# A graph layer's source rows: one tile in 64 fetched row by row by SyncE instead of by an indirect DMA of GpSimd

## The chip, the cores and the metric

One core of a Trainium2 chip. The metric is the device time of one execution in microseconds, the median of several; beside it stands one profiled execution with its trace.

## What is computed

One message-passing layer over a graph of 12,500 nodes (64 features) and 212,500 edges (32 features), sorted by destination, with a residual and a layer norm. All is float32:

```python
msg_in = concatenate([nodes[row], nodes[col], edge_features], axis=-1)
messages = relu(msg_in @ mW1 + mb1) @ mW2 + mb2
aggregated = segment_sum(messages, col, num_segments=12500)
upd = relu(concatenate([nodes, aggregated]) @ uW1 + ub1) @ uW2 + ub2
out = layernorm(nodes + upd)
```

`row` (the kernel's `src`) is in no order; `col` (`dst`) rises along the edges. So what belongs to the destinations lies in a narrow window of nodes for a stretch of edges, and what belongs to the sources has to be gathered.

## The kernel before

The edges are cut into 554 groups (G) of 384 edges, three tiles of 128 each (TG = 3). Of each group the kernel needs the source rows x[src], one edge to a partition, in `own_s`, a ring of RING = 20 groups in SBUF; the edge features in `own_st`, transposed, one block to four groups (SB = 4); and a window of 32 rows of a table of destinations (`by_dst`, made on the chip in the first steps) in `own_wm`, a ring of eight.

The loop over k (lines 617 to 662) is one step of a software pipeline. TensorE does three things in step k as one block of matmuls, with one wait ahead of it (`step`, line 586):
- `turn(k)` (372): it transposes the three tiles of group k from `own_s` into PSUM (L378). It waits for the group's gathers and for the one-hot columns. ScalarE then copies the result into `own_st` (L389).
- `hidden(k-2)` (399): the first layer of the messages (L404), from `own_st` and `own_wm`; VectorE takes the relu into `own_h` (L415).
- `sums(k-4)` (425): the segment sums by one-hot matmuls (L431), and counts (L442); VectorE adds them into `agg` (L458) and `xc` (L463).

The order on each engine is the order in which the code calls for it; nothing is rescheduled. The engines meet through semaphores alone.

The source rows come in two ways. **GpSimd** issues one indirect DMA per tile (`gather`, line 164, L167), 16 groups ahead in the order of the code. Before it overwrites a slot of the ring it waits for the transpose of the group that had the slot (`turn_by[g - RING]`). It has no other work in the loop. **VectorE and ScalarE** spare it the first tile of 180 groups (COPIED): they copy single columns of 64 features from x^T, which lies whole in SBUF, into `own_st`, 20 columns a step on VectorE (L565) and 24 on ScalarE (L567), at addresses loaded into registers (L546) from a list of indices (L525). So a group has three gathers or, one time in three, two: 1481 in all.

**SyncE** issues the other DMAs from one queue, in order, and an instruction that waits holds up all behind it. In step k these are, in this order: every fourth step the edge features of a later block (`inputs`, 312, L316), which wait for the step k-1 of TensorE; the output of a finished block of nodes, one step in 21 or so (L516), which waits for VectorE; `window(k + 4)` (347), the rows of `by_dst` for group k+4 at an address from a register (L358; every fourth step it loads four registers first, L353), which waits for TensorE's step k-2; every eighth step a list of column indices (L525). Until step 24 it also writes `by_dst`, block by block (L344).

Of the kernel before, what the change touches and what calls it, by code (L numbers as in the profile page):

```python
# [12 lines left out]
I32 = mybir.dt.int32  # L13
# [3 lines left out]
ET = mybir.EngineType  # L17
# [3 lines left out]
P = 128  # L21
N = 12500
E = 212500
D = 64
# [6 lines left out]
TG = 3  # L31
GE = TG * P
G = (E + GE - 1) // GE
SB = 4
AHEAD = 16
RING = AHEAD + 4
BLOCKS = 3
NW = 2 * SB
COUNT = 96
# [7 lines left out]
SHORT = 10  # L47
LEAD = 6
TIMES = 4
BEGIN = 18  # L50
# [2 lines left out]
ACOLS = (12, 12)  # L53
COLS = sum(VCOLS + ACOLS)
SPAN = 8


def tiles_of(g):

    n = min(GE, E - g * GE)  # L60
    return [min(P, n - j * P) for j in range((n + P - 1) // P)]
# [23 lines left out]
COPIED = []  # L85
while BEGIN - (-P * (len(COPIED) + 1) // COLS) < G - SHORT:
    COPIED.append(BEGIN - (-P * (len(COPIED) + 1) // COLS))


class Own:  # L90
# [24 lines left out]
def ordered(ctx: ExitStack, tc: tile.TileContext, a, own, ok):  # L115
# [3 lines left out]
    nc = tc.nc  # L119
    x, out = a["x"], a["out"]  # L120
# [5 lines left out]
    ixp = ctx.enter_context(tc.tile_pool(name="index", bufs=2))  # L126
# [10 lines left out]

    loads, places_by, copy_by, relu_by, sums_by, wm_by, turn_by = ({} for _ in range(7))
    efs_by, hidden_by, counted_by = {}, {}, {}
    columned = set(COPIED)  # L140

    def after(first, *others):

# [20 lines left out]
    def gather(g):  # L164
        s = own.s[g % RING]
        loads[g] = [
            nc.gpsimd.indirect_dma_start(  # L167
                out=s[:p, j, :D], out_offset=None, in_=x[:, :],
                in_offset=bass.IndirectOffsetOnAxis(
                    ap=src_sb[:p, g * TG + j : g * TG + j + 1], axis=0),  # L170
            )
            for j, p in enumerate(tiles_of(g)) if j or g not in columned
        ]
        for i in loads[g]:
            after(i, *([turn_by[g - RING]] if g >= RING else []))

# [93 lines left out]
    wc = const.tile([H, H], F32, name="wc")  # L270

    starts, rows_at, indices, columns_by = {}, {}, {}, {}
    by_dst = dram.tile([NP, H], F32, name="by_dst")
    written = []

# [71 lines left out]
    def window(g):  # L347

        if g >= G:
            return  # L350
        if g % SB == 0:
            n = min(SB, G - g)
            _, v = nc.values_load_multi_w_load_instructions(  # L353
                start_i[0:1, g : g + n], engines=[ET.SP], min_val=0, max_val=N - 1,
                skip_runtime_bounds_check_because="they were clamped to the nodes on the chip",
            )
            rows_at.update(zip(range(g, g + n), v))
        wm_by[g] = nc.sync.dma_start(wm[g % NW][D : D + W, :],  # L358
                                     by_dst[bass.ds(rows_at.pop(g), W), :])
        after(wm_by[g], *written, *([hidden_by[g - NW]] if g >= NW else []))  # L360
        written.clear()
# [10 lines left out]
    def turn(g, ps):  # L372


        s = own.s[g % RING]
        xt = ps[0][: D + W, :GE]
        did = [
            nc.tensor.transpose(xt[:, j * P : j * P + p], s[:p, j, :], ident[:p, :p])  # L378
            for j, p in enumerate(tiles_of(g))
        ]  # L380

        def copy(step):
            t, c, n = columns(g)
            turn_by[g] = step
            whole = [(slice(D + W), slice(n))]
            apart = [(slice(D, D + W), slice(P)), (slice(D + W), slice(P, n))]
            copies = [
                ordered_by_steps(
                    after(nc.scalar.activation(t[r, c : c + n][:, m], xt[r, m], AF.Copy), step))  # L389
                for r, m in (apart if g in columned else whole)  # L390
            ]
            if g >= BLOCKS * SB:
                after(copies[0], hidden_by[g - BLOCKS * SB])
            copy_by[g] = copies
            return copies

        return did, [*loads.pop(g), places_by[g]], copy

    def hidden(g, ps):
        t, c, n = columns(g)  # L400
# [67 lines left out]
    def update(base, p, n):  # L468

        rows, q = slice(base, base + p * n), p * n  # L470

        def inner():
            u_ps = ups.tile([H, CH], F32, name="u_ps")
            nc.tensor.matmul(u_ps[:, :q], wc, agg[:, rows], start=True, stop=False)
            nc.tensor.matmul(u_ps[:, :q], ux, xc[: COUNT + 1, rows], start=False, stop=True)
            return u_ps

        def relu(u_ps):
            u = up.tile([H, CH], F32, name="u")
            nc.scalar.activation(u[:, :q], u_ps[:, :q], AF.Relu)  # L480
            return u

        def outer(u):
            y = ups.tile([H, CH], F32, name="u_ps")[:, : 4 * D].rearrange("p (n d) -> p n d", n=4)
            for k in range(n):
                at = k * p
                nc.tensor.matmul(y[:p, k], xc[: D + 1, base + at : base + at + p], same,  # L487
                                 start=True, stop=False)
                nc.tensor.matmul(y[:p, k], u[:, at : at + p], u2, start=False, stop=True)  # L489
            return y  # L490

        def stats(y):
            parts = up.tile([P, 4, nc.vector.BN_STATS_DIM], F32, name="stats")
            mv = up.tile([P, 4, nc.vector.BN_AGGR_DIM], F32, name="mv")
            for k in range(n):
                nc.vector.bn_stats(parts[:p, k], y[:p, k])
                nc.vector.bn_aggr(mv[:p, k], parts[:p, k])
            return y, mv

        def root(ym):  # L500
            y, mv = ym
            rstd = up.tile([P, 4], F32, name="rstd")
            nc.scalar.activation(rstd[:p, :n], mv[:p, :n, 1], AF.Sqrt, bias=eps[:p])
            return y, mv, rstd

        def scaled(ymr):
            y, mv, rstd = ymr
            nc.vector.reciprocal(rstd[:p, :n], rstd[:p, :n])
            o = up.tile([P, 4, D], F32, name="o")
            for k in range(n):  # L510
                nc.vector.tensor_scalar(
                    o[:p, k], y[:p, k], mv[:p, k, 0:1], rstd[:p, k : k + 1],
                    ALU.subtract, ALU.mult,
                )
            queue = nc.scalar if base + q == N else nc.sync
            queue.dma_start(out[rows, :].rearrange("(n p) d -> p n d", p=p), o[:p, :n])  # L516

        return [inner, relu, outer, stats, root, scaled]

    def indexes(i):  # L520

        n = min(SPAN * COLS, P * len(COPIED) - i * SPAN * COLS)
        if n > 0:
            indices[i] = ixp.tile([1, SPAN * COLS], I32, name="index")
            nc.sync.dma_start(indices[i][:, :n], a["src_copied"][:, i * SPAN * COLS :][:, :n])  # L525

# [26 lines left out]
    def fetch(*parts):  # L553

        for part in parts:
            engine, c0, v = held.pop(part, (None, 0, ()))
            for q, at in enumerate(v, c0):
# [8 lines left out]
                else:  # L566
                    by[engine] = nc.scalar.activation(o, x_at, AF.Copy)  # L567
                ordered_by_steps(after(by[engine],
                                       *([hidden_by[g - BLOCKS * SB]] if new else [])))

    waiting = [(closes, update(base, p, n)) for base, p, n, closes in PLAN]
    now = []

# [37 lines left out]
    for g in range(SB):  # L611
        window(g)
    indexes(0)
    made = summed = 0
    between, held = [], {}

    for k in range(G):
        if k < BITS:
            bit(k)
        if 1 < k < len(TABLE):  # L620
            projected(k)
        if k == CHECKED:
            addresses(0)
            combined()
            ordered_edges()
            early.close()
            up = ctx.enter_context(tc.tile_pool(name="upd", bufs=2))
        if k % SB == 2:
            inputs(k // SB + 2)
        if k % SB == 1:  # L630
            places(k // SB + 1)
        if k < G - SHORT:
            between.append(lambda: registers(k, 0))
            step((turn, k), *([(hidden, k - 2)] if k > 1 else []),
                 *([(sums, k - 4)] if k > 3 else []))
            made, summed = max(0, k - 1), max(0, k - 3)
            if between:
                between.pop()()
            fetch(0)
        else:  # L640

            step((turn, k))
            for _ in range(2):
                if summed < made:
                    step((sums, summed))
                    summed += 1
            for _ in range(2):
                if made <= k:
                    step((hidden, made))
                    made += 1  # L650
        window(k + SB)
        onehot(k + LEAD)
        if k < G - SHORT:
            for part in range(1, len(VCOLS + ACOLS)):
                registers(k, part)
                fetch(part)
            if k >= BEGIN and (k - BEGIN) % SPAN == 0:
                indexes((k - BEGIN) // SPAN + 1)
            if k >= BEGIN and (k - BEGIN) % SPAN == SPAN - 2:
                addresses((k - BEGIN) // SPAN + 1)  # L660
        if k + AHEAD < G:
            gather(k + AHEAD)
# [330 lines left out]
```

## Time and profile before

| | us |
|---|---|
| median of 3 runs | 1879.1 (1875.58 to 1879.48) |
| the profiled execution | 1872.44 |
| its span, first to last instruction | 1870.6 |

Busy shares of that span: TensorE's matmuls 70%, its weight loads 61%, VectorE 78%, ScalarE 83%, GpSimd 75%; mean granted TensorE clock 0.952. The 16 DMA engines were busy for a quarter of the time through most of the span. How to read it: no engine is near 100%, since each has gaps that the page lists as idle time with what ended them; issuing a DMA, loading registers and waiting on SyncE count as no busy time at all, so SyncE has no row among the engines and must be looked up in the waits, by source line and in the timeline.

### The profile page before, as it was taken

To read this page: it belongs to the slowest core of one execution; us is meant where nothing else is said; L and a number is where in the kernel's file an instruction comes from. 1 tells how busy PE (TensorE), PEld (TensorE's weight loads), DVE (VectorE), ACT (ScalarE), POOL (GpSimd) and SP (SyncE) were. 2 spreads that over 40 slices of the span, in tenths; PEclk is the share of its full clock that TensorE was granted. 3 is DMA by queue.
4 is the path that set the end of the run, shared out by engine and by line. 5 is a ranking of instruction groups with operands and counts; after the bars stand their busy time and mean duration, and the time that the engine had idled before them with its cause. 6 is when DMAs were issued, how large, how long until landed. Compare 5 with 4: busy or idle time off the path is not lost. (4 is left out here: it accounts for less than half of the span.)

```text
span 1870.6 us, 55967 instructions
## 1 busy us (share of the span) xinstructions
PE 1302.0 (70%) x9839; PEld 1139.3 (61%) x9839; DVE 1452.9 (78%) x13141; ACT 1558.7 (83%) x13374; POOL 1400.1 (75%) x1488
## 2 busy tenths in 40 slices
PE   1777777677767667677676776776767767667676
PEld 0676666666666556566665666665656656556665
DVE  1338888899897888877887878888878888888773
ACT  5249999999998888888888888888888888888871
POOL 7777777777777777777777777777777777777774
PEclk9889999999999998998999998999998999999999
DMA  4543222222222222222222222222222222222221
GB/s 93 138 123 75 54 54 54 51 54 53 52 54 48 50 52 49 50 49 45 54 52 47 52 46 54 48 51 48 53 46 53 45 54 51 48 53 48 50 49 26
DMA packets 112796, 104.10 MB, mean 56 GB/s; under 512 B 51586, under 2 KB 82960, under 8 KB 112432
## 3 DMA queue, kind: packets, MB, share of 16 engines
q0 software_dynamic: 47392, 48.60, 14.8%
q1 hardware_dynamic: 64196, 51.35, 10.0%
q14 instruction: 280, 2.29, 0.4%
q8 instruction: 84, 1.38, 0.3%
q10 hardware_dynamic: 844, 0.48, 0.1%
HBM read 90.61 MB, written 9.62 MB: 54 GB/s over the span
## 5 line engine op out<-in xcount | busy, mean ns | idle before, releaser
L167 POOL DMA_INDIRECT own_s<-in_x,src_sb x1481 | 1399.4, 945 | 452.5 <-issue 342.9
L567 ACT ACTIVATE own_st<-own_xc 64x4 uint8 x12560 | 1265.6, 192 | 60.2 <-issue 52.2
L565 DVE COPY own_st<-own_xc 64x4 uint8 x10480 | 884.5, 190 | 17.3 <-issue 9.2
L378 PE MATMUL own_ps<-own_ident,own_s 128*96 128x128 f32 x1661 | 294.1, 288 | 488.7 <-DMA own_s<-in_x,src_sb 164.0
L378 PEld LDWEIGHTS own_ps<-own_ident,own_s 128*96 128x96 f32 x1661 | 169.1, 131 | 593.5 <-issue 291.0
L431 PE MATMUL own_ps<-own_s,own_h 128*128 128x128 f32 x3322 | 490.3, 287 | 1.2 <-DVE own_h L415 0.6
L404 PE MATMUL own_ps<-own_wm,own_st 128*128 128x128 f32 x3322 | 485.5, 285 | 0.0
L415 DVE TENSOR_SCALAR own_h<-own_ps 128x384 f32<-128x384 f32 x553 | 302.1, 547 | 185.5 <-PE own_ps L442 84.7
L431 PEld LDWEIGHTS own_ps<-own_s,own_h 128*128 128x128 f32 x3322 | 443.3, 203 | 2.3 <-DVE own_h L415 1.2
L404 PEld LDWEIGHTS own_ps<-own_wm,own_st 128*128 128x128 f32 x3322 | 437.8, 201 | 1.8 <-issue 1.2
L389 ACT ACTIVATE own_st<-own_ps 96x384 f32<-96x384 f32 (+2 forms) x734 | 294.2, 401 | 167.5 <-PE own_ps L442 81.6
L458 DVE TENSOR_TENSOR own_agg<-own_ps,own_agg 128x32 f32 x554 | 105.8, 191 | 170.6 <-DVE own_h L415 90.4
L366 DVE TENSOR_TENSOR own_s<-iota,dlc 128x96 f32<-128x96 f32 x554 | 136.2, 247 | 0.3 <-issue 0.2
L442 PE MATMUL own_ps<-own_s,own_one 128*1 128x128 f32 x834 | 120.6, 283 | 0.0
L463 DVE TENSOR_TENSOR own_xc<-own_ps,own_xc 1x32 f32 x554 | 101.9, 184 | 18.5 <-DVE own_xc L463 1.8
L442 PEld LDWEIGHTS own_ps<-own_s,own_one 128*1 128x1 f32 x834 | 60.2, 85 | 35.7 <-issue 3.6
L340 PE MATMUL u_ps<-w1b,own_xc 65*128 65x128 f32 x196 | 33.4, 323 | 58.1 <-ACT t L343 38.8
L340 PEld LDWEIGHTS u_ps<-w1b,own_xc 65*128 65x128 f32 x196 | 29.1, 227 | 62.3 <-ACT t L343 42.1
L343 ACT ACTIVATE t<-u_ps 128x512 f32<-128x512 f32 (+1 forms) x25 | 14.7, 588 | 58.2 <-DMA by_dst<-t 37.9
L487 PE MATMUL u_ps<-same,own_xc 65*128 65x64 f32 (+1 forms) x196 | 37.0, 271 | 1.5 <-ACT u L480 1.4
L489 PE MATMUL u_ps<-u,u 128*128 128x64 f32 (+1 forms) x196 | 38.0, 276 | 0.0
L487 PEld LDWEIGHTS u_ps<-same,own_xc 65*128 65x128 f32 (+1 forms) x196 | 29.7, 191 | 2.3 <-ACT u L480 2.2
(62 smaller groups left out, 257.1 us busy)
## 6 DMA issues: line engine op xcount, KB each, us to landing
own_st<-in_efT SPq DMA_DIRECT2D x138, 192.0 KB
own_s<-in_x,src_sb POOLq DMA_INDIRECT x1481
own_wm<-by_dst SPq DMA_DIRECT2D x554, 16.0 KB
by_dst<-t SPq DMA_DIRECT2D x24, 256.0 KB
out<-o SPq DMA_DIRECT2D x24, 128.0 KB
own_xc<-in_xT SPq DMA_DIRECT2D x12, 179.2 KB
index<-in_src_copied SPq DMA_DIRECT2D x65, 1.4 KB
dlc_i<-in_dst_cols SPq DMA_DIRECT2D x1, 831.0 KB
```

Of the source, the lines that this page charges most:

```text
L167: nc.gpsimd.indirect_dma_start(out=s[:p, j, :D], out_offset=None, in_=x[:, :], in_offset=bass.IndirectOffsetOnAxis(ap=src_sb[:p, g * TG + ...
L366: places_by[g] = nc.vector.tensor_tensor(own.s[g % RING][:, :, D:], iota.unsqueeze(1).to_broadcast([P, TG, W]), dlc[:, g * TG : (g + 1) * ...
L378: nc.tensor.transpose(xt[:, j * P : j * P + p], s[:p, j, :], ident[:p, :p])
L389: after(nc.scalar.activation(t[r, c : c + n][:, m], xt[r, m], AF.Copy), step))
L404: nc.tensor.matmul(pre[:p, j, :], t[:, c + j * P : c + j * P + p], wm[g % NW], start=True, stop=True)
L415: relu_by[g] = [nc.vector.tensor_scalar(h, pre, 0.0, None, ALU.max)]
L431: did.append(nc.tensor.matmul(sg, h[:p, j, :], s[:p, j, D:].unsqueeze(1).to_broadcast([p, TIMES, W]), start=j == 0, stop=j == len(sizes) - 1))
L442: did.append(nc.tensor.matmul(at_ps[:, : len(whole)], own.one, own.ring[:, first_s : first_s + len(whole), j, D:], start=j == 0, stop=j == ...
L458: did = [after(nc.vector.tensor_tensor(agg[:, at], sg[:, 0, :], agg[:, at], ALU.add), step)]
L463: did.append(after(nc.vector.tensor_tensor(count, counted, count, ALU.add), step))
L565: by[engine] = nc.vector.tensor_copy(o, x_at)
L567: by[engine] = nc.scalar.activation(o, x_at, AF.Copy)
```

## The change

Of 24 groups (41, 62, 83, 105, ..., 531: BY_ROWS) the last tile is no longer gathered by GpSimd. SyncE fetches its 128 rows, 256 bytes each, one DMA to a row, six in a step (ROWS_A_STEP), from step 18 on. The group whose rows were issued last in some step is used two steps later (ROW_LEAD). The address of each row comes from a register; every second step SyncE loads twelve registers (PAIR) from a list of indices, which is fetched anew every 16 steps. In step k all of this comes behind `window(k + 4)`. The first row of a group waits for the transpose of the group that had the slot; as rows of one group are fetched over 21 to 22 steps ahead, the ring goes from 20 to 24 groups. The transposes of such a group wait for its rows too. In the built program each row is a pair of an address calculation and a DMA, as each fetch of `window` is, and the order of the other instructions on SyncE stays.

```diff
-RING = AHEAD + 4
+RING = 24
...
+ROWS_A_STEP = 6
+PAIR = 2 * ROWS_A_STEP
+ROW_SPAN = 8 * PAIR
+ROW_LEAD = 2
...
+BY_ROWS = []
+while True:
+    last = BEGIN + (P * (len(BY_ROWS) + 1) - 1) // ROWS_A_STEP
+    if last + ROW_LEAD >= G - SHORT:
+        break
+    BY_ROWS.append(last + ROW_LEAD)
...
-            for j, p in enumerate(tiles_of(g)) if j or g not in columned
+            for j, p in enumerate(tiles_of(g))
+            if (j or g not in columned) and (j < TG - 1 or g not in by_rows)
...
-        return did, [*loads.pop(g), places_by[g]], copy
+        return did, [*loads.pop(g), *rows_by.pop(g, []), places_by[g]], copy
...
+    def row_indexes(i):
+
+        n = min(ROW_SPAN, P * len(BY_ROWS) - i * ROW_SPAN)
+        if n > 0:
+            row_index[i] = ixp.tile([1, ROW_SPAN], I32, name="row_index")
+            nc.sync.dma_start(row_index[i][:, :n], a["src_rows"][:, i * ROW_SPAN :][:, :n])
+
+    fetched = []
+
+    def row_numbers(k):
+
+        q, odd = divmod(k - BEGIN, 2)
+        if k < BEGIN or odd:
+            return
+        i, b = divmod(q * PAIR, ROW_SPAN)
+        n = min(PAIR, P * len(BY_ROWS) - q * PAIR)
+        if n > 0:
+            _, v = nc.values_load_multi_w_load_instructions(
+                row_index[i][0:1, b : b + n], engines=[ET.SP], min_val=0, max_val=N - 1,
+                skip_runtime_bounds_check_because="a source is one of the nodes",
+            )
+            fetched.extend(enumerate(v, q * PAIR))
+        if b == ROW_SPAN - PAIR:
+            row_indexes(i + 1)
+
+    def row_fetch():
+
+        for q, node in [fetched.pop(0) for _ in fetched[:ROWS_A_STEP]]:
+            g, p = BY_ROWS[q // P], q % P
+            i = nc.sync.dma_start(
+                own.s[g % RING][p : p + 1, TG - 1, :D].rearrange("p (a b) -> p a b", a=2),
+                x[bass.ds(node, 1), :].rearrange("p (a b) -> p a b", a=2))
+            after(i, *([turn_by[g - RING]] if g >= RING and not p else []))
+            rows_by.setdefault(g, []).append(i)
+
...
         window(k + SB)
+        row_numbers(k)
+        row_fetch()
         onehot(k + LEAD)
```

More of the change, by code (lines that the diff above doesn't have):

```diff
@@ L139, in ordered @@
     efs_by, hidden_by, counted_by = {}, {}, {}
-    columned = set(COPIED)
+    columned, by_rows = set(COPIED), set(BY_ROWS)
     def after(first, *others):
@@ L272, in ordered @@
     starts, rows_at, indices, columns_by = {}, {}, {}, {}
+    rows_by, row_index = {}, {}
     by_dst = dram.tile([NP, H], F32, name="by_dst")
@@ L613, in ordered @@
     indexes(0)
+    row_indexes(0)
     made = summed = 0
@@ L974 @@
         "src_copied": np.concatenate([v["src"][g * GE :][:P] for g in COPIED])[None],
+        "src_rows": np.concatenate([v["src"][g * GE + GE - P :][:P] for g in BY_ROWS])[None],
         "dst_cols": padded(v["dst"], G * TG * P, -1).reshape(G * TG, P).T,
```

## The prediction

> **What bounds the kernel now.** I read the page's groups first, then the busy time by stretches for two lines (the gathers, and TensorE's transposes, of which every group has three), and last the waits. The gathers stand at the top of the groups:
>
> ```profile
> span 1870.6 us, 55967 instructions
> ...
> L167 POOL DMA_INDIRECT own_s<-in_x,src_sb x1481 | 1399.4, 945 | 452.5 <-issue 342.9
> ```
>
> Busy 1399.4 us with 452.5 us idle before them is 1851.9 us, all of the span but 19 us: 0.945 us of work and 0.31 us until the next, mostly "issue", which is waiting for nothing. GpSimd never stands still. That alone doesn't make it the bound; who keeps pace with it does. Line L167 in stretches of the span (length, busy time, count), then L378:
>
> ```profile
> 220.00:371.00 151.00, 114.20 (x121) 0.99 0.25 52
> 371.00:681.00 310.00, 234.30 (x248) 0.97 0.24 52
> 681.00:1013.00 332.00, 251.23 (x266) 0.94 0.24 50
> ```
> ```profile
> 220.00:371.00 151.00, 26.16 (x153) 15.08 (x153) 0.99 0.25 52
> 371.00:681.00 310.00, 52.02 (x300) 30.02 (x300) 0.97 0.24 52
> 681.00:1013.00 332.00, 53.42 (x300) 30.14 (x300) 0.94 0.24 50
> ```
>
> GpSimd gives one gather per 332/266 = 1.248 us in each stretch. TensorE does 51 groups in 151 us (2.96 us a step), then 100 in 310 (3.10), then 100 in 332 (3.32). It starts behind, catches up, and from about 680 us on it has GpSimd's rate: 266 gathers for 100 groups is 2.66 x 1.248 = 3.32. So there are two limits: GpSimd at 3.32 us a step, and below it the loop of PE, ACT and DVE, which has shown 2.96. The waits agree, TensorE's on the gathers and then SyncE's own:
>
> ```profile
> PE own_ps L378 <- DMA own_s<-in_x,src_sb: 164.0, 133, 2.6
> ```
> ```profile
> SPq L316 <- PE own_ps L431: 521.4, 108, 6.7
> SPq L516 <- DVE o L511: 264.7, 23, 13.7
> SPq L358 <- PE own_ps L442: 240.2, 95, 5.7
> ```
>
> SyncE spends over 1000 us waiting for engines that are behind it. This slack is what the change spends.
>
> **What it removes.** 24 groups (41, 62, ... 531) lose one gather of three: 24 x 1.248 = 30 us of GpSimd. Its rate would be (1481 - 24) x 1.248 / 554 = 3.28 us a step, still above 2.96, so if nothing else became late all 30 us would come off the end: 1870.6 - 30 = 1841 us of span.
>
> **What it adds to SyncE.** From step 18 on, for 24 x 128 = 3072 rows, 512 steps long, each step issues six DMAs of one row, each with an address from a register, and every second step loads twelve registers. The nearest rows are those of the node-table fetch (L358), which also has its address in a register, the small index load (L525, one partition), the edge features (L316) and the register loads. First, count and min/median/max in ns:
>
> ```profile
> L358 SPq FUSED_REGOPS  x554: 37/37/51, 39.8 to 1830.3; - x185
> L358 SPq MOVE own_wm<-by_dst x554: 29/29/38, 41.2 to 1830.4; - x185
> L358 SPq DMA_DIRECT2D own_wm<-by_dst x554: 315/316/1517, 41.3 to 1830.6; - x185
> L358 SPq EVENT_SEMAPHORE  x279: 17/17/1846, 39.9 to 1830.4; - x140
> ...
> L525 SPq DMA_DIRECT2D index<-in_src_copied x66: 269/270/308, 43.2 to 1778.4; - x66
> ...
> L316 SPq DMA_DIRECT2D own_st<-in_efT x139: 321/322/740, 22.1 to 1826.0; - x139
> ...
> L353 SPq TENSOR_LOAD <-start_i x139: 293/315/743, 39.2 to 1827.3; - x139
> ...
> L328 DVEq TENSOR_LOAD <-start_i x139: 340/344/650, 12.1 to 1840.5; - x139
> ...
> L546 DVEq TENSOR_LOAD <-index x1048: 591/843/1125, 123.6 to 1817.6; - x175
> L546 ACTq TENSOR_LOAD <-index x1047: 549/782/1358, 123.6 to 1814.8; - x175
> ```
>
> and SyncE's order of time, for what lies between two issues:
>
> ```profile
> 1005.35 0.32 SPq L316 DMA_DIRECT2D own_st<-in_efT  x1
> 1005.87 0.32 SPq L358 DMA_DIRECT2D own_wm<-by_dst  x1
> 1008.95 0.28 SPq L525 DMA_DIRECT2D index<-in_src_copied  x1
> 1009.42 1.42 SPq L358 DMA_DIRECT2D own_wm<-by_dst  x2
> ```
>
> From the end of one DMA to the start of a register-addressed one behind it are 1005.87 - 1005.67 = 0.20 and 1009.42 - 1009.23 = 0.19 us: FUSED_REGOPS, MOVE and the gaps around them. The instruction itself took 0.27 us for the one-partition load and 0.32 us for 32 rows. A row fetch moves one row in two halves, so it is nearest to the first: 0.19 + 0.27 = **0.46 us**; I keep 0.51 us (the 32-row fetch) as the upper end. No DMA of SyncE's in these rows took under 0.269 us, so the lower end is soft: 0.42 if the two halves cost less than any row shown, and 0.19, the address alone, as the floor that nothing can pass.
>
> Twelve registers: DVE's 4 cost 0.344 and its larger load 0.843, ACT's twelve 0.782; SyncE's 4 cost 0.315, so 0.315 + (0.843 - 0.344) = 0.81, take 0.80 (0.55 to 0.85 as ends).
>
> SyncE's step, without any wait, from these rows (0.05 us is the gap behind an instruction, 0.06 an extra semaphore instruction):
> - six rows: 6 x 0.46 = 2.76
> - twelve registers: (0.80 + 0.05) / 2 = 0.43, and their index load every 16 steps 0.02
> - node-table fetch: 0.32 + 0.19 + half of 0.06 = 0.54
> - its registers: (0.315 + 0.05) / 4 = 0.09
> - edge features: (0.32 + 0.05 + 0.06) / 4 = 0.11
> - column indices: 0.45 / 8 = 0.06; output: 0.45 / 21 = 0.02
>
> Before it is 0.82 us a step; after it is 4.03, take **4.0 us**. GpSimd needs 3.28 and the compute loop 2.96. So SyncE, idle for three quarters of a step before, becomes the slowest engine, by a fifth. Nothing hides that: its lead of a few steps is used up within some ten steps, since it loses 0.7 us or more in each.
>
> **How the lateness reaches the end.** Rows of group g are issued up to step g-2, and the transpose of step g waits for all of them. Queued behind the rows on SyncE are the node-table fetch (four groups ahead of its group, whose matmul comes two steps later, so it may be six steps late) and the edge features (eight steps), so the rows are late first. I expect TensorE to stop at each of the 24 groups until SyncE has ended step g-2 and the last row has landed, then to run at 2.96 us a step for about 21 steps, gaining 21 x 1.04 = 22 us, and to stop again. SyncE's waits for engines vanish: at a stop TensorE is two steps ahead of SyncE, later more, and every wait of SyncE's asks for a step at or before its own.
>
> **The sum.** SyncE's rows begin at step 18, behind the fetch at 133.06:
>
> ```profile
> 133.06 0.33 SPq L358 DMA_DIRECT2D own_wm<-by_dst  x1
> 133.44 0.30 SPq L525 DMA_DIRECT2D index<-in_src_copied  x1
> 134.93 0.41 SPq L344 DMA_DIRECT2D by_dst<-t  x1
> 137.27 0.32 SPq L358 DMA_DIRECT2D own_wm<-by_dst  x1
> ```
>
> In steps 18 to 24 SyncE also writes a block of the node table and waits for its landing: 137.27 - 134.93 = 2.3 us, less the 0.2 of the fetch's addresses, 2.1. Seven steps of 4.0 + 2.1 are 43 us: step 25 at 133 + 43 = 176. Then 505 steps x 4.0 = 2020: the last row is issued at 2196. A landing: the chain shows 1.3 us for the index load and 2.4 for a gather, take 2.
>
> ```profile
> 1751.45 1.29 DMA index<-in_src_copied
> 1771.39 2.45 DMA own_s<-in_x,src_sb
> ...
> L167 POOL DMA_INDIRECT own_s<-in_x,src_sb x1481: 901/944/1667, 3.0 to 1852.5; - x186
> ```
>
> After group 531 come 22 steps; their gathers are long done (GpSimd is up to 24 groups ahead), so 22 x 2.96 = 65. The drain: the last gather starts at 1852.5, lands 0.94 + 2.45 later, and the span ends at 1870.6: 14.7. Span: 2196 + 2 + 65 + 15 = 2278; the profiled execution took 1872.4 for its 1870.6, so 2280. The median shown, 1879.1, is 6.7 us above that execution; against a change of 400 us I leave this out.
>
> **What costs nothing.** The ring of 24 only lets GpSimd run four groups further ahead and gives a row its slot 23 steps before its use; its waits on the transposes were already short, and a longer wait of GpSimd's is behind SyncE's. PE gets some more semaphores to wait for at 24 groups, under 0.1 us each by the EVENT_SEMAPHORE row. The rows are 3072 x 256 bytes, 0.8 MB of the 104 MB moved.
>
> **Rivals.**
> 1. *Heavier rows* (chance 0.15). The row costs what the 32-row fetch does (0.51), or needs a semaphore instruction of its own (0.06) because the landing it waits for isn't in yet (SyncE's DMAs take eight semaphores in turn, and each waits for the landing of the eighth before it). Against the latter: eight DMAs are 3.7 us, more than a landing. Steps of 4.3 to 4.65 us, that is 176 + 505 x 4.3 + 82 = 2430 up to 2610. [...]
> 2. *Lighter rows* (0.09). 0.38 to 0.42 us a row, below any row shown: steps of 3.5 to 3.75 us, 2030 to 2150 us.
> 3. *SyncE keeps up and GpSimd's 30 us are gained* (0.05): 1841 + 2 = 1843 us. It decides where the step of SyncE passes GpSimd's 3.28: a row must cost (3.28 - 1.27) / 6 = 0.33 us or less, so its DMA instruction 0.14 us, half of the shortest in the trace. For it speaks that no DMA this small with two halves is in the trace. [...]
> 4. *Even* (0.02): a row of 0.34 to 0.35 us, where SyncE's 3.3 is what GpSimd's was.
>
> **How the numbers follow.** The forecast, steps of 3.8 to 4.3 us, has 0.69 and gives 2280. The range leaves out rival 3, 4, most of 2 and the dear half of 1: 2150 (3.75 us a step) to 2450 (4.33). A measurement of this kernel tells about 0.2% from no change. Faster by more than that: rival 3, 0.05. Within: 0.02. Slower: 0.93.
>
> **What would show it.** Right: about 3072 row DMAs on SyncE of 0.27 to 0.32 us, 256 register loads near 0.8; SyncE's waits for PE and DVE, over 1000 us before, nearly gone after 180 us; 100 groups per 400 us in the middle stretches; TensorE's wait for own_s<-in_x in some 20 stops of 15 to 25 us; GpSimd with 1457 gathers and now waiting for PE. Wrong: SyncE still waiting for PE each step (rival 3), TensorE stopped by the node-table fetch rather than the rows (then the slack is other than I count), or row DMAs that wait for each other's landing (rival 1).

## The result and the profile after

The changed kernel takes 2238.5 us (median of 4 runs, 2237.2 to 2242.8) where the kernel before takes 1877.7 (4 runs): a ratio of 1.193, 95% interval 1.190 to 1.195. It was forecast at 2280, range 2150 to 2450. The profiled execution has a span of 2235.4 us.

In the views PE is TensorE, PEld its weight loads, POOL GpSimd, DVE VectorE, ACT ScalarE and SPq SyncE's queue; a wait has its total in us, how often it came and the longest. The stretches of TensorE's transposes (line 378 before, 390 now; length, busy time and count, weight loads, granted clock, DMA share, GB/s) give the pace:

```profile
1013.00:1413.00 400.00, 54.66 (x300) 31.25 (x300) 0.85 0.20 42
1413.00:1813.00 400.00, 54.95 (x306) 31.83 (x306) 0.87 0.21 43
```

That is 100 and 102 groups in 400 us, 4.0 and 3.92 us a step, where 3.32 stood before. The groups and GpSimd's waits show that GpSimd isn't the bound any more:

```profile
L177 POOL DMA_INDIRECT own_s<-in_x,src_sb x1457 | 1376.8, 945 | 765.3 <-issue 378.3
```
```profile
POOL own_s L177 <- DMA own_s<-in_x: 158.1, 21, 16.8
POOL own_s L177 <- PE own_ps L443: 96.7, 32, 16.8
```

24 gathers are gone as planned, each still takes 945 ns, but the idle time before them went from 452.5 to 765.3 us: GpSimd now has filled the ring and waits for TensorE to free a slot. The first of these waits is put down to the rows, but it ends only behind TensorE's next block of matmuls: in one of these stops TensorE starts again at 1066.50 us and GpSimd at 1070.06. TensorE in turn waits for the rows:

```profile
PE own_ps L390 <- DMA own_s<-in_x: 431.1, 23, 20.7
PE own_ps L390 <- DMA own_wm<-by_dst: 89.7, 57, 2.7
```

These are 23 stops of 18.7 us on average, the longest 20.7, where 24 groups take their rows from SyncE. The twenty-fourth, of 18.1 us, the view puts down to an index load. But it ends at 2152.51 us, 1.8 us after the last row was issued and only 0.44 us after that index load was, so the rows are the likelier cause. Last SyncE itself. Its waits, longest first, were 521.4, 264.7 and 240.2 us before:

```profile
SPq L370 <- DMA by_dst<-t: 46.0, 24, 2.8
SPq L528 <- DVE own_agg L470: 26.1, 2, 25.7
SPq L528 <- DVE o L523: 20.2, 5, 10.8
...
SPq L328 <- PE own_ps L443: 11.5, 6, 4.9
```

Little is left but the first of them, which belongs to the steps up to 24, and the 25.7 us of the second, which lie behind the last row. Between them SyncE works almost without a break. This is how it does, in order of time:

```profile
1000.25 2.33 SPq L612 DMA_DIRECT2D own_s<-in_x  x6
1002.83 0.32 SPq L370 DMA_DIRECT2D own_wm<-by_dst  x1
1003.34 2.62 SPq L612 DMA_DIRECT2D own_s<-in_x  x6
1006.07 0.33 SPq L328 DMA_DIRECT2D own_st<-in_efT  x1
1006.59 0.66 SPq L370 DMA_DIRECT2D own_wm<-by_dst  x1
1008.41 2.33 SPq L612 DMA_DIRECT2D own_s<-in_x  x6
1010.92 0.32 SPq L370 DMA_DIRECT2D own_wm<-by_dst  x1
```

Six rows take 2.3 to 2.6 us, or one (2.33 - 0.23) / 5 = 0.42, and the 1.2 us between 1007.25 and 1008.41 hold the load of twelve registers. From one fetch of the node table to the next are 3.8 and 4.3 us. The rows by source line (count, min/median/max in ns, first and last start in us):

```profile
L612 SPq FUSED_REGOPS  x3072: 37/37/42, 132.4 to 2150.6; - x192
L612 SPq MOVE own_s<-in_x x3072: 29/29/29, 132.5 to 2150.7; - x192
L612 SPq DMA_DIRECT2D own_s<-in_x x3072: 224/228/279, 132.6 to 2150.7; - x192
...
L600 SPq TENSOR_LOAD <-row_index x256: 747/761/951, 131.7 to 2144.3; - x128
...
L365 SPq TENSOR_LOAD <-start_i x139: 300/558/746, 39.2 to 2196.1; - x139
...
L537 SPq DMA_DIRECT2D index<-in_src_copied x66: 231/234/313, 43.1 to 2152.1; - x66
...
L588 SPq DMA_DIRECT2D row_index<-in_src_rows x32: 234/269/280, 43.5 to 2078.8; - x32
```

In the first comparison below (e1 to e4) every kernel, that of before too (2473 us), ran some 600 to 750 us longer, for a cause that isn't known, so there only ratios between its kernels can be read, and all four were run again.

### The profile page after: what moved, and what is told of

Its sections match the earlier page's. It is cut to its first block, busy times and chain, and to the rows that moved or that the text cites. A ratio compares the mean times of both kernels' runs of the same rounds, so it can differ in the third digit from the quotient of the medians.

```text
span 2235.4 us, 65560 instructions
## 1 busy us (share of the span) xinstructions
PE 1323.0 (59%) x9839; PEld 1163.5 (52%) x9839; DVE 1444.7 (65%) x13141; ACT 1541.4 (69%) x13374; POOL 1377.6 (62%) x1464
## 5 line engine op out<-in xcount | busy, mean ns | idle before, releaser
L177 POOL DMA_INDIRECT own_s<-in_x,src_sb x1457 | 1376.8, 945 | 765.3 <-issue 378.3
L390 PE MATMUL own_ps<-own_ident,own_s 128*96 128x128 f32 x1661 | 302.1, 294 | 821.7 <-DMA own_s<-in_x 431.1
L390 PEld LDWEIGHTS own_ps<-own_ident,own_s 128*96 128x96 f32 x1661 | 175.6, 134 | 918.9 <-issue 756.9
L416 PE MATMUL own_ps<-own_wm,own_st 128*128 128x128 f32 x3322 | 498.1, 290 | 0.0
L416 PEld LDWEIGHTS own_ps<-own_wm,own_st 128*128 128x128 f32 x3322 | 451.4, 206 | 1.9 <-issue 1.2
L443 PEld LDWEIGHTS own_ps<-own_s,own_h 128*128 128x128 f32 x3322 | 448.1, 205 | 6.1 <-DVE own_h L427 4.4
```

The costliest lines, as they stand in the source:

```text
L177: nc.gpsimd.indirect_dma_start(out=s[:p, j, :D], out_offset=None, in_=x[:, :], in_offset=bass.IndirectOffsetOnAxis(ap=src_sb[:p, g * TG + ...
L416: nc.tensor.matmul(pre[:p, j, :], t[:, c + j * P : c + j * P + p], wm[g % NW], start=True, stop=True)
L443: did.append(nc.tensor.matmul(sg, h[:p, j, :], s[:p, j, D:].unsqueeze(1).to_broadcast([p, TIMES, W]), start=j == 0, stop=j == len(sizes) - 1))
```

## The experiments

The theory: SyncE's own time per step, 3.92 us, one instruction behind the other, is the whole cause (**issue**). The rivals: the rows are asked for too late, and with more lead SyncE would do (**lateness**); the small transfers themselves, their landing or their packets between those of the gathers (**transfer**); the larger ring.

### The ring alone: e1_ring24 and e11_ring24_again

```diff
-RING = AHEAD + 4
+RING = 24
```

> The kernel before with the ring of 24 groups and nothing else. Issue theory (SyncE's serial issue time of 3.92 us a step is the whole cause): the ring costs nothing, 1877 us, within 0.3% of the kernel before. If the larger ring itself cost something (the gathers running further ahead), it would be slower by some of the 360 us; above 1890 us would say so.

> The ring of 24 alone, once more, since 0.6% was seen where GpSimd wasn't the bound. With GpSimd as the bound: the same as the kernel before within 0.3%, since GpSimd has no wait on the ring to lose.

Measured: 1873.0 us beside 1872.9, ratio 1.0003 (0.9993 to 1.0013). In the first comparison the ratio was 1.0063 (1.0035 to 1.0091). In the trace of that run (e1) GpSimd was idle for 984 us in its four longest waits alone and so was no bound; what made the 0.6% stays open. Where GpSimd is the bound, the ring costs nothing.

### The same DMAs without registers: e2_const and e5_const_again

```diff
-            _, v = nc.values_load_multi_w_load_instructions(row_index[i][0:1, b : b + n], ...)
+            v = range(q * PAIR, q * PAIR + n)
...
-                x[bass.ds(node, 1), :].rearrange("p (a b) -> p a b", a=2))
+                x[node : node + 1, :].rearrange("p (a b) -> p a b", a=2))
```

> The changed kernel with the row addresses as constants (row q of x for the q-th fetch) in place of registers, so it gathers wrong source rows for 24 tiles; number, size, order and destination of the row DMAs and their lead stay. Issue theory: a SyncE step loses 0.45 us of register loads, 0.02 us of their index loads and six times 0.142 us of address instructions, 3.92 - 1.32 = 2.60 us, which is under GpSimd's 3.28, so the kernel is bound by GpSimd again and the 24 gathers saved show: 1848 us (1843 to 1865). Transfer rival (the landing of 3072 small DMAs, or their packets between the gathers' packets, holds things up): same DMAs, so still some 2200 us. Lateness rival (SyncE would keep up, but two steps' lead is too short for the rows): the stops of TensorE remain for the most part, over 2000 us.

> The kernel with constant row addresses (wrong source rows in 24 tiles) once more, since in the first comparison every kernel, that of before too, took some 600 us longer than its trace of before and GpSimd was no longer its bound. Issue theory: SyncE's step 2.60 us, GpSimd the bound, the 24 gathers saved show: 1848 us (1843 to 1865). Transfer and lateness rivals: over 2000 us.

Measured: 1843.1 us beside 1872.8, ratio 0.985 (0.983 to 0.986); in the first comparison 2500 beside 2473, ratio 1.012 (1.004 to 1.020), where GpSimd was no bound and nothing could be gained from it; why it was slower there stays open. So 3072 DMAs of 256 bytes, issued at the same places and as short a time ahead, cost nothing once SyncE can issue them within a step, and the 24 gathers bring what they were priced at: 29.7 us for 24 x 1.248 = 30. The transfer and the lateness rival fall, with one thing open: these constant rows lie one behind the other in memory, and the real ones are scattered. The runs with fewer rows, below, close that. SyncE has time to wait again, GpSimd has none, and what TensorE waits for most is the gathers. SyncE's waits, then TensorE's, then GpSimd's:

```profile
SPq L528 <- DVE o L523: 143.7, 22, 10.4
SPq L328 <- PE own_ps L443: 61.7, 34, 6.2
```
```profile
PE own_ps L390 <- DMA own_s<-in_x,src_sb: 111.5, 88, 2.7
...
PE own_ps L390 <- DMA own_s<-in_x: 77.3, 42, 7.6
```
```profile
POOL own_s L177 <- issue: 334.9, 1098, 0.3
```

A row is now its DMA instruction alone:

```profile
L608 SPq DMA_DIRECT2D own_s<-in_x x3072: 219/251/416, 132.9 to 1744.0; - x192
```

TensorE still waits 77 us for rows, up to 7.6 us at once, and almost none of that shows in the time: it makes it up before the gathers notice.

### Rows that nobody waits for: e3_unused and e10_unused_again

```diff
-            if (j or g not in columned) and (j < TG - 1 or g not in by_rows)
+            if j or g not in columned
...
-                own.s[g % RING][p : p + 1, TG - 1, :D].rearrange("p (a b) -> p a b", a=2),
+                own.rows[q // P % ROW_BUFS][p : p + 1, :].rearrange("p (a b) -> p a b", a=2),
...
-        return did, [*loads.pop(g), *rows_by.pop(g, []), places_by[g]], copy
+        return did, [*loads.pop(g), places_by[g]], copy
```

> SyncE fetches the same rows at the same addresses, but into two buffers that nothing reads; GpSimd gathers all 1481 tiles as before, the transposes don't wait for the rows, the ring is 20 again. Issue theory: SyncE's 3.92 us a step still sets the pace, now through the node-table fetch, which may be six steps late; the last row is issued near 2150 us, and TensorE is at step 534 then, so 20 steps of 3 us and a drain of 15 us follow: 2227 us (2210 to 2245). Lateness rival and the landing half of the transfer rival: nobody waits for a row, so 1878 us.

> The rows fetched into buffers that nothing reads, all 1481 gathers kept, once more. Issue theory: SyncE's 3.92 us a step sets the pace through the node-table fetch, 2227 us (2210 to 2245). Lateness rival, and the landing half of the transfer rival: 1873 us, as the kernel before.

Measured: 2213.5 us beside 1872.9, ratio 1.182 (1.178 to 1.185); in the first comparison 1.200. With no engine waiting for a row the loss stays: 341 us for 361. TensorE waits in its place for what is queued on SyncE behind the rows, the node-table fetch, not in 24 long stops but in 361 short ones:

```profile
PE own_ps L392 <- DMA own_wm<-by_dst: 579.0, 361, 3.6
```

### More lead: e4_lead8 and e8_lead8_again

```diff
-RING = 24
+RING = AHEAD + 4
...
-ROW_LEAD = 2
+ROW_LEAD = 8
+ROW_BUFS = 2
...
+        self.rows = [on(f"own_rows{i}", P, D + W) for i in range(ROW_BUFS)]
...
+        if g in by_rows:
+            n = BY_ROWS.index(g)
+            i = nc.vector.tensor_tensor(
+                own.rows[n % ROW_BUFS][:, D:].unsqueeze(1),
+                iota.unsqueeze(1),
+                dlc[:, g * TG + TG - 1 : (g + 1) * TG].unsqueeze(2).to_broadcast([P, 1, W]),
+                ALU.is_equal,
+            )
+            after(i, *([turn_by[BY_ROWS[n - ROW_BUFS]]] if n >= ROW_BUFS else []))
...
-            nc.tensor.transpose(xt[:, j * P : j * P + p], s[:p, j, :], ident[:p, :p])
+            nc.tensor.transpose(
+                xt[:, j * P : j * P + p],
+                own.rows[BY_ROWS.index(g) % ROW_BUFS] if j == TG - 1 and g in by_rows
+                else s[:p, j, :], ident[:p, :p])
...
-                own.s[g % RING][p : p + 1, TG - 1, :D].rearrange("p (a b) -> p a b", a=2),
+                own.rows[q // P % ROW_BUFS][p : p + 1, :D].rearrange("p (a b) -> p a b", a=2),
...
-            after(i, *([turn_by[g - RING]] if g >= RING and not p else []))
+            after(i, *([turn_by[BY_ROWS[q // P - ROW_BUFS]]] if q >= P * ROW_BUFS and not p else []))
```

> The changed kernel with the rows issued eight steps ahead of use in place of two; for room, the rows go to two buffers of their own, with a one-hot of their own (one VectorE instruction more in 24 steps), and the ring is 20. Issue theory: the pace is the same 3.92 us a step; the last stop of TensorE is six steps nearer to the end (group 537), which saves six steps of 3 us: 2220 us (2205 to 2240), and the stops move from the rows to the node-table fetch. Lateness rival: the stops go, 1850 to 1900 us.

> Six rows a step, eight steps ahead, once more. Issue theory: the same 3.92 us a step as with two steps' lead, the last stop six steps nearer to the end: 2220 us (2205 to 2240), the stops at the node-table fetch. Lateness rival: 1850 to 1900 us.

Measured: 2223.3 us beside 1872.8, ratio 1.187 (1.185 to 1.190); in the first comparison 1.195. The pace by the stretches of its transposes is the 3.92 us of before, and TensorE's stops have moved to the node-table fetch, as in the run before:

```profile
681.00:1073.00 392.00, 55.86 (x300) 30.89 (x300) 0.90 0.19 42
```
```profile
PE own_ps L401 <- DMA own_wm<-by_dst: 567.5, 350, 3.6
```

This queue, too slow for its work, is late with whatever stands in it; a longer lead only chooses what.

### Fewer rows: e6_r4, e7_r5, e9_r5_load12, e12_r4_lead2

On the kernel with eight steps of lead, one number changes (`ROWS_A_STEP`), with it the number of relieved groups.

```diff
-ROWS_A_STEP = 6
+ROWS_A_STEP = 4
```

> Four rows a step instead of six, so 16 groups instead of 24 are relieved; rows in their own two buffers, issued eight steps ahead, ring 20. Issue theory: SyncE's step is 0.94 + 0.02 + 4 x 0.423 + 0.30 = 2.95 us, under GpSimd's 3.30, so 16 x 1.248 = 20 us are gained: 1858 us (1853 to 1872). If SyncE's in-order waits (for the output of VectorE, for TensorE's step) take more than the 0.35 us a step that it has to spare, it is late after each of them and TensorE stops again: 1880 to 1950 us. Transfer rival: two thirds of the 360 us, some 2115 us.

> The same with five rows a step, 20 groups relieved. Issue theory: SyncE's step is 0.96 + 5 x 0.423 + 0.37 = 3.45 us, just over GpSimd's 3.28; the last row is issued near 168 + 505 x 3.45 = 1910, TensorE is up to five steps ahead, 20 steps of 3 us and 15 us of drain follow: 1985 us (1945 to 2015). Transfer rival: five sixths of the 360 us, some 2180 us.

Four rows: 1852.8 us beside 1872.8, ratio 0.990 (0.988 to 0.991). 20.0 us are gained, as many as 16 gathers of 1.248 us, and SyncE waits again:

```profile
SPq L542 <- DVE o L537: 92.0, 15, 10.1
SPq L372 <- DMA by_dst<-t: 44.3, 24, 2.9
SPq L330 <- PE own_ps L457: 30.7, 25, 7.0
```

Five rows: 2201.9 us, ratio 1.176 (1.173 to 1.178), where 1985 was expected. The sum of SyncE's step was wrong here by one term. The register load by its source line, first of four rows a step (eight registers), then of five (ten):

```profile
L614 SPq TENSOR_LOAD <-row_index x256: 521/540/728, 133.1 to 1750.4; - x128
```
```profile
L614 SPq TENSOR_LOAD <-row_index x256: 967/1612/2097, 134.8 to 2123.6; - x128
```

Ten registers cost about 1.13 and 2.08 us in turn, while twelve took 0.75 and 0.94; the pace was 606 transposes, or 202 groups, in 784 us, 3.88 us a step:

```profile
681.00:1073.00 392.00, 57.86 (x306) 31.93 (x306) 0.90 0.19 43
1073.00:1465.00 392.00, 56.28 (x300) 30.94 (x300) 0.90 0.20 43
```

So the next run kept five rows and loaded twelve registers, two of them unused, from a list laid out in twelves (the main lines):

```diff
-ROW_SPAN = 8 * PAIR
+HELD = 12
+ROW_SPAN = 8 * HELD
...
-                row_index[i][0:1, b : b + n], engines=[ET.SP], min_val=0, max_val=N - 1,
+                row_index[i][0:1, b : b + HELD], engines=[ET.SP], min_val=0, max_val=N - 1,
```

> Five rows a step as before, but the list of row numbers is laid out in twelves (ten used, two of padding) and twelve registers are loaded instead of ten. In the run with ten, the sum of SyncE's step missed by the register load alone: ten registers took 1.13 and 2.08 us in turn, 0.83 us a step, where twelve took 0.75 and 0.94, 0.45 us a step. Theory (the load's length or alignment, ten numbers at steps of 40 bytes, is what was dear; the sum of the step holds otherwise): twelve take 0.75 to 0.95 us again, the step is 3.88 - 0.83 + 0.45 = 3.50 us and the time 168 + 505 x 3.50 + 76 = 2012 us (1990 to 2035). Rival (with five rows a step something else than the count makes the load slow, such as what SyncE does around it): loads stay above 1.1 us, 2200 us.

Measured: 2002.2 us, ratio 1.069 (1.067 to 1.071). Two registers more, and 200 us less: the load is back, and the step is 897 transposes, or 299 groups, in 1044 us, 3.49 us.

```profile
L615 SPq TENSOR_LOAD <-row_index x256: 747/762/953, 131.1 to 1927.0; - x128
```
```profile
681.00:1029.00 348.00, 50.77 (x297) 28.37 (x297) 0.97 0.21 48
1029.00:1377.00 348.00, 52.72 (x299) 30.14 (x300) 0.95 0.21 47
1377.00:1725.00 348.00, 52.77 (x301) 29.71 (x300) 0.95 0.22 48
```

So one sum, SyncE's step against GpSimd's 3.3, tells gain from loss in each of these: 2.95 us and a gain with four rows (the sum in the expectation, an estimate), 3.49 and a loss with five, 3.88 with five and the dear load, 3.92 with six. These runs fetch the real, scattered rows. With ten registers or with twelve the rows are the same 2560, and 200 us lie between; with four a step 2048 of them cost nothing. So neither their number nor their being scattered is the cause. Is it the lead, then, that lets four rows gain?

> Four rows a step with the lead of two steps instead of eight, all else as in the kernel with four rows. Issue theory: SyncE has 0.35 us a step to spare, so the pace is GpSimd's; a stop of TensorE for rows that come late behind an output's wait is made up again, since TensorE is faster than GpSimd: 1853 us, within 0.3% of the kernel with eight. If the lead matters here: 16 stops of up to 3 us that aren't made up, up to 1900 us.

Measured: 1855.1 us, ratio 0.990 (0.988 to 0.992): the same gain with two steps. TensorE stops for late rows, and makes it up:

```profile
PE own_ps L401 <- DMA own_rows<-in_x: 66.7, 20, 14.7
```

Four rows a step is the version with the right rows that beats both kernels, by 1.0% of the one before.

## Why the prediction was right

- **GpSimd the bound before, the loop of PE, ACT and DVE close below.** Right: with the rows made cheap, the 24 gathers gave 29.7 us for the 30 of the prediction, and GpSimd was at its limit again.
- **SyncE's step, 4.0 us.** Right, 3.92, with two errors of opposite sign. Added up from the trace between 400 and 2100 us, each instruction with the gap behind it, the rows take 2.54 us of a step (predicted 2.76), the twelve registers 0.45 (0.43) and the rest 0.93 (0.84).
  - A row was priced 0.46 us, "nearest to" the small index load of 0.27. Its DMA instruction took 0.228 and the whole row 0.42. That is the dear edge of rival 2, to which the prediction gave 0.09. By the row alone the step would have been 3.8 us and the time near 2180, still within the range. That the dearer rest brought the number closer is luck.
  - The lower end had been called soft, and the shortest DMA of the trace of before was not a floor. In the trace of after a row that follows another DMA within some 0.2 us takes 0.228 us in the median, and more than 2,700 of the 3072 do. A row that comes behind the load of twelve registers, some 1.2 us after the DMA before it, takes 0.27. The index load itself took 0.270 in the median before; now it comes right behind a row and takes 0.234, while the other index load (L588), which has a register load ahead of it, takes 0.269. Why the price differs isn't shown: 13 of the 66 index loads of before came 0.11 to 0.13 us behind a node-table fetch (one at 162.11, behind the fetch of 0.32 us at 161.68) and took 0.27 all the same. In the trace each row is also one piece of 256 bytes (15,360 packets of that size, 12,288 before), not the two halves that the prediction reckoned with.
  - The rest was dearer mostly through the load of four registers, 0.558 us in the median where the trace of before had 0.315.
- **Twelve registers, 0.80 us.** Right: 0.75 and 0.94 in turn, 0.845 on average.
- **Start and end.** The first row was issued at 132.6 and the last at 2150.7, predicted near 134 and 2196; 505 steps of 0.08 us less are 40 of these 45 us, and of the 42 us by which 2280 is over 2238. From the last row to the end are 84.7 us, predicted 82.
- **What is late first.** Right: the rows, in 23 stops of 18.7 us for "some 20 stops of 15 to 25". Five sixths of TensorE's two waits on SyncE's DMAs are theirs. The rest, 89.7 us for the node-table fetch between the stops, the prediction had put at nothing. e8 and e10 showed that it takes over where the rows are early or unused.
- **The rivals.** Rival 3 named its point of decision, a row of 0.33 us or less, and e5 is it: with constant addresses there is only the DMA, 0.251 us in the median (0.30 with the 0.05 that the prediction counts for the gap behind an instruction), and no register load; the step fits, and the 30 us appear. With addresses in registers a row's 0.42 us is still less than the 1.3 to 2.0 us from the issue of a group's last row to TensorE's start; but the issues follow one another, and six of them take 2.5 of the 3.3 us of a step. Rival 1's waits for the landing of the eighth DMA before didn't come. In the trace of after 3,953 of 3,956 DMAs of SyncE's carry the semaphore of the eighth before them, but only 38 rows in 3072 have a semaphore instruction of their own, of 0.017 to 0.028 us, and no row's DMA took more than 0.279 us.
- **The ring.** Nothing, as predicted: e11.

## What to carry to other kernels

Before work is moved to an engine that looks idle, add up that engine's whole step from the trace, with address calculations, register loads and the gaps between instructions, and hold it against the pace of the bound: here 3.9 against 3.3 us lost 360 us, 2.95 gained 20. SyncE's queue, over its time, was late with the rows or with the node-table fetch behind them, so neither more lead (e8, 1.187) nor dropping the wait (e10, 1.182) helped here; only less work per step did (e6, 0.990). Once the queue fitted, TensorE's stops for rows (77.3 us in all in e5, 66.7 in e12) cost almost nothing, and the move paid what it took off the bound: 29.7 us for 30, and 20.0 for 20.

## What the runs showed of the hardware

- A load of registers on SyncE took 0.54 us in the median for eight (e6, 0.521 to 0.728) and 0.75 or 0.94 in turn for twelve (the kernel after), but 1.13 or 2.08 in turn for ten at steps of 40 bytes (e7). Whether the count or the address made ten dear wasn't tried apart; that both of two tens are dearer than twelve, and one of them by far, leads the author to suspect both. Loads of four took 0.300 us at the least in the kernel after.
- A small DMA instruction had no one price on SyncE. In the kernel after, rows within some 0.2 us of the DMA before them took 0.228 us in the median and rows behind a register load 0.27; the index load took 0.270 us in the median before and 0.234 after. The pause since the DMA before doesn't settle it alone, since 13 index loads of before had a pause of 0.11 to 0.13 us and took 0.27; no run varied the pause.
- With TensorE waiting in 24 long stops, its granted clock was 0.85 to 0.87 in the middle stretches, for 0.94 to 0.97 before. With 350 short stops for the node-table fetch, 568 us in all (e8), it was 0.90 to 0.92; with 305, 425 us in all (e9), 0.95 to 0.97. What sets it wasn't tried, and what it cost can't be told here, since SyncE set the pace.
